# Two graph layers on one core: queries and keys by fifteen block products, and attention under the products around it

## The chip, the core and the metric

The kernel runs on one core of a Trainium2 chip. The core has five engines that run side by side and wait for each other by semaphores: TensorE (PE, matmuls and transposes), VectorE (DVE), ScalarE (ACT), GpSimd (POOL) and SyncE (SP), which issues nearly all the DMA transfers here. Each engine takes its instructions strictly in order, so an instruction that waits holds up all that stand behind it on its engine. The metric is the device time of one execution in microseconds (us); lower is better.

## The reference, cut to what matters

128 graphs have 64 nodes each, with 768 features and an adjacency matrix per graph, all in fp32. Two layers follow each other, each with a residual and a layer norm.

```python
# layer 0: graph attention, 12 heads of 64, and a gate
h    = x @ W                                   # all heads side by side, 768 x 768
th   = tanh(h)
attn = th @ w_src + (th @ w_dst).T             # per head, 64 x 64
attn = softmax(where(adj, leaky_relu(attn, 0.2), -999))
y    = elu(attn @ h + b)
gate = sigmoid(x @ H_w.T + H_b)
x    = layernorm(x + gate * y + (1 - gate) * x)
# layer 1: attention inside a graph, 6 heads of 128
q, k, v = x @ Wq + bq, x @ Wk + bk, x @ Wv + bv
p    = softmax(q @ k.T / sqrt(128) + where(adj, 0, -9e15))
x    = layernorm(x + (p @ v) @ Wf + bf)
```

The 8192 tokens thus pass through six products with a 768 x 768 matrix: h, gate, v, q, k and the output. The change is to q and k, and to the attention of layer 1.

## The kernel before

**Block products.** A product of tokens with a 768 x 768 matrix is cut into blocks of two by two by two. Eight block products would be plain; a Winograd scheme makes do with seven, from sums of blocks of the rows (`block_sums`, L184 to L197) and of the weights (`weight_sums`, L165 to L172). `Job` (L199 to L247) is one such product. `product(i)` issues block product i as three matmuls (its 384 rows of contraction, 128 at a time) into a PSUM bank, some of them onto what is in the bank already; `way_out(i)` reads the bank, by ACT where a result is written first (`first`, `last`) and by DVE where it is added (`add`). `step` (L257) issues a product, then the way out of the product before, so that the reads run one product behind.

**First layer.** Tokens go by pairs of tiles of 128 (32 pairs). The loop at L880 runs one turn per pair, 21 products a turn written out in order (`TURN`, L77): seven for h, seven for the gate, seven for v of the pair before. Everything else of a turn is hung onto positions of that list by `at` and `was` (L891 to L938). The chain through a turn is: h out of PSUM, tanh (L660), its product with the two attention vectors (L661 on DVE, L662 on POOL), a reduction (L669), a round trip through DRAM that turns one of the results into a row (L671, L674), and the logits, mask and exponentials of the 12 heads (L698 to L731), whose transposes stand at the start of the next turn. v waits for row sums of the normed tokens (L192 to L195 on DVE), and the next turn's h and gate for row sums on POOL.

**Passage.** In the last turns (`p == NP - 1`, L940, and `LAST`, L66) the query and key weights are loaded into the places of the first layer's weights as their blocks fall free, and their sums are made on POOL and DVE. `queries_begin` (L870) gives the space of the first layer's rows to the second layer and loads the first group's rows.

**Second layer.** Tokens go by groups of four tiles (512 tokens, 8 graphs; 16 groups). Queries and keys of a group come transposed, features on the partitions. There are three `feature_job`s (L324) per key and group, `fc` = 0 to 2. Each makes 128 features of the lower half and 128 of the upper half, for 512 tokens, in seven products of three matmuls of 256 columns: 63 matmuls per key and group. `attention` (L345) does two heads, those that a feature job has made. It is a generator and goes on one step at each product of the pair of jobs that runs meanwhile (`woven`, L513): load of the values, scores `sp` (16 small matmuls), bias and maximum (L375, L383), exponential, sum and division (L390 to L393), transposes `sT`, context `cp` (32 small matmuls), copy to `ctxT`. A group's loop (L1000 to L1029) has the three pairs of query and key jobs, then the pair of output jobs of the group before. The row sums of a group's tokens are four of 768 columns on POOL (`load_group`, L300). `residuals` (L436) loads the first layer's result, adds the output bias on POOL (L457) and makes the row sums for the output products; `finish` (L497) norms and stores.

There is no scheduler: the order of instructions on each engine is that of the code. A PSUM bank is 128 x 512 fp32; three carry the tag `y`, three `z`, and two `m` (attention and transposes).

Of the kernel before, what the change touches and what calls it, by code (L numbers as in the profile page):

```python
# [9 lines left out]
F32 = mybir.dt.float32  # L10
# [5 lines left out]
P = 128  # L16
# [45 lines left out]
    0: 7, 1: 7, 2: 8, 3: 9, 4: 10, 5: 11, 6: 12, 7: 12, 8: 13, 9: 14, 11: 15, 12: 15, 15: 16, 16: 17, 19: 19,  # L62
# [3 lines left out]
LAST = [  # L66
    "u4", "u3", "q1", "q2", "k1", "k2", "q6", "q5", "q7", "Q1", "q4", "Q2", "q3", "k6", "k5", "k7",
    "Q6", "k4", "k3", "v1", "v2", "v6", "v5", "v7", "K1", "v4", "v3",
]
LAST_REST = [(1, 2), (0, 5), (1, 6), (0, 7), (1, 5), (1, 7), (0, 4), (0, 3), (1, 4), (1, 3)]  # L70
LAST_AT = {3: 3, 4: 4, 5: 6, 6: 8, 7: 9, 8: 11, 9: 12, 11: 15, 12: 16, 15: 20, 16: 20, 19: 22}
# [10 lines left out]
THIRD_AT = {pos: max(pos - 2, 0) for pos in range(len(TURN))}  # L82
# [8 lines left out]
def kernel(  # L91
# [24 lines left out]
    SCALE = 1.0 / math.sqrt(E1)  # L116

# [16 lines left out]
    dst_d = [dram.tile([P, H0], F32, name=f"dstd_{t}") for t in range(2 * NP)]  # L134

# [152 lines left out]
    W2 = PAIR * P  # L288
# [4 lines left out]
    qk, groups = {}, {}  # L293

    def query_tiles(g, fc):
        qk[g, fc] = [
            pools["early"].tile([P, 2, GT * P], F32, tag=f"{k}T", name=f"{k}T_{g}_{fc}") for k in "qk"
        ]

    def load_group(g, eng, between=lambda: None):  # L300

        pool = pools["early"]
        sums = sum_tiles(pool, "sq", W2, f"q{g}")
        between()
        blocks = {}
        for m, kh in ((0, 0), (1, 0), (1, 1), (0, 1)):
            t = pool.tile([P, HK, W2], F32, tag=f"a{m}{kh}", name=f"a{m}{kh}_{g}", bufs=1)
            nc.sync.dma_start(out=t, in_=x1T_d[2 * g + m][:, kh * HK : (kh + 1) * HK, :])
            blocks[m, kh] = t
        groups[g], steps = block_sums(eng, sums, *(blocks[m, kh] for m in range(2) for kh in range(2)))  # L310
        return steps

    def feature_jobs(g, fc):
        return [feature_job(k, groups[g], g, fc, t) for k, t in zip("qk", qk[g, fc])]
# [9 lines left out]
    def feature_job(key, ops, g, fc, dst):  # L324

        w, b = weights[key], bias_c[key]

        def at(m, n):
            return dst[:, n, m * W2 : (m + 1) * W2]

        def bias(n):
            return b[:, n * HK + fc : n * HK + fc + 1]

        return Job(
            f"{key}{g}_{fc}",
            W2,
            lambda i, kc: (w[:, OF_B[i], kc, fc * P : (fc + 1) * P], ops[i][:, kc, :]),
            lambda mn, bk_: S.activation(at(*mn), bk_, AF.Identity, bias=bias(mn[1])),  # L338
            lambda mn, bk_: V.tensor_tensor(at(*mn), bk_, at(*mn), ALU.add),  # L339
            lambda bk_: S.activation(at(1, 0), bk_, AF.Identity, bias=bias(0)),  # L340
        )

    ctxT = {}

    def attention(g, fc, bias):  # L345

        sb = pools["late"]
        qT, kT = qk.pop((g, fc))

        v = sb.tile([P, GT, 2, E1], F32, tag="v1", name=f"v1_{g}_{fc}")  # L350
        for a in range(2):
            c0 = (a * J1 + fc) * E1
            for i in range(GT):
                nc.sync.dma_start(
                    out=v[a * N : (a + 1) * N, i, :, :],
                    in_=v_d[GT * g + i][:, c0 : c0 + E1].rearrange("(g m) e -> m g e", m=N),
                )
        yield
        yield
        yield  # L360
        sp = bank("m", f"sp_{g}_{fc}")
        for i in range(GT):
            for a in range(2):
                for gr in range(2):
                    at = slice(i * P + gr * N, i * P + (gr + 1) * N)
                    T.matmul(
                        sp[gr * N : (gr + 1) * N, (i * 2 + a) * N : (i * 2 + a + 1) * N],
                        qT[:, a, at],
                        kT[:, a, at],
                        start=True,  # L370
                        stop=True,
                    )
        yield
        sc = sb.tile([P, GT, 2, N], F32, tag="sc", name=f"sc_{g}_{fc}")
        V.tensor_tensor(  # L375
            sc,
            sp.rearrange("p (i a m) -> p i a m", i=GT, a=2),
            bias.unsqueeze(2).to_broadcast([P, GT, 2, N]),
            ALU.add,
        )  # L380
        sc3 = sc.rearrange("p i a m -> p (i a) m")
        mx = small.tile([P, 2 * GT], F32, tag="mx1", name=f"mx1_{g}_{fc}")
        V.tensor_reduce(mx, sc3, AX.X, ALU.max)  # L383
        yield
        V.tensor_tensor(sc3, sc3, mx.unsqueeze(2).to_broadcast([P, 2 * GT, N]), ALU.subtract)  # L385
        S.activation(sc, sc, AF.Exp, scale=SCALE)  # L386
        yield
        yield
        den = small.tile([P, 2 * GT], F32, tag="den1", name=f"den1_{g}_{fc}")
# [46 lines left out]
    def residuals(g, last):  # L436
# [14 lines left out]
        if last:  # L451
            sums = sum_tiles(early, "sq", W2, f"o{g}")
# [634 lines left out]
```

## Time and profile before

| | |
|---|---|
| median of 3 runs | 2970.18 us (2967.41 to 2971.54) |
| the profiled execution, its own time | 2970.77 us |
| its span in the profile | 2969.0 us |
| mean granted clock of TensorE | 0.995 |
| PE, DVE, ACT, POOL busy | 2925.2, 1796.9, 1009.0, 811.1 us |
| a turn of the first layer | 45.6 us |
| a group of the second layer | 90.5 us |

The profile is of one execution. Its lines name the source line, the engine, the operation, what is written and what is read (out<-in), how often, and how long. Every fp32 matmul leaves two records, so x576 stands for 288 matmuls. In a group's line the first number after the bar is busy time in us, the second the mean of one in ns, and after the second bar stands the idle time of the engine just before, with what ended it. Line numbers are those of the kernel before.

### The profile page before, as it was taken

To read this page: it belongs to the slowest core of one execution; us is meant where nothing else is said; L and a number is where in the kernel's file an instruction comes from. 1 tells how busy PE (TensorE), PEld (TensorE's weight loads), DVE (VectorE), ACT (ScalarE), POOL (GpSimd) and SP (SyncE) were. 2 spreads that over 40 slices of the span, in tenths; PEclk is the share of its full clock that TensorE was granted. 3 is DMA by queue.
4 is the path that set the end of the run, shared out by engine and by line. 5 is a ranking of instruction groups with operands and counts; after the bars stand their busy time and mean duration, and the time that the engine had idled before them with its cause. 6 is when DMAs were issued, how large, how long until landed. Compare 5 with 4: busy or idle time off the path is not lost.

```text
span 2969.0 us, 45314 instructions
## 1 busy us (share of the span) xinstructions
PE 2925.2 (99%) x18048; PEld 2023.0 (68%) x18048; DVE 1796.9 (61%) x3017; ACT 1009.0 (34%) x1761; POOL 811.1 (27%) x650
## 2 busy tenths in 40 slices
PE   7999999999999999999999999999999999999999
PEld 4566666666666666666578777787777887777875
DVE  6878888788788878887844344333343443443345
ACT  2344344444443444444422222222222222222221
POOL 2434333333343333333422212211111212121121
PEclk9999999999999999999999999999999999999999
DMA  5333333334333333343532211222212222112221
GB/s 171 122 109 114 107 121 115 103 118 128 104 119 104 121 113 106 115 129 103 176 97 77 70 60 55 86 86 76 68 52 64 86 76 73 59 57 82 87 80 48
DMA packets 179681, 284.81 MB, mean 96 GB/s; under 512 B 46736, under 2 KB 113296, under 8 KB 179472
## 3 DMA queue, kind: packets, MB, share of 16 engines
q1 hardware_dynamic: 179472, 281.93, 29.1%
q8 instruction: 143, 2.34, 0.3%
q14 instruction: 66, 0.54, 0.1%
HBM read 167.81 MB, written 101.06 MB: 91 GB/s over the span
## 4 chain that ended last, share of the span: by engine, by line
PE 94%; DVE 3%; DMA 1%; ACT 1%; issue 0%; SPq 0%; POOLq 0%; POOL 0%; DVEq 0%; ACTq 0%
PE y_k L222 8%; PE y_o L222 8%; PE y_q L222 8%; PE y_v L222 8%; PE y_h L222 8%; PE y_g L222 8%; PE z_v L222 4%; PE z_o L222 4%; PE z_k L222 4%; PE z_h L222 4%; PE z_q L222 4%; PE z_g L222 4%; PE x_k L222 2%; PE x_o L222 2%; PE x_q L222 2%; PE x_h L222 2%
## 5 line engine op out<-in xcount | busy, mean ns | idle before, releaser
L789 POOL TENSOR_TENSOR x<-gate,x 128x768 f32<-128x768 f32 x64 | 117.4, 1835 | 323.8 <-ACT gate L840 309.0
L457 POOL TENSOR_TENSOR y<-y,bf_bc 128x768 f32<-128x768 f32 x64 | 115.3, 1832 | 311.4 <-DMA y<-x1d 311.4
L481 DVE TENSOR_TENSOR y<-y_o,y 128x384 f32<-128x384 f32 x128 | 71.4, 557 | 202.1 <-PE y_o L222 198.0
L339 DVE TENSOR_TENSOR kT<-z_k,kT 128x256 f32<-128x256 f32 x96 | 40.8, 425 | 239.3 <-PE z_k L222 136.1
L662 POOL TENSOR_TENSOR th<-th,wsd 128x768 f32<-128x768 f32 x64 | 117.2, 1832 | 182.5 <-DVE th L661 182.5
L274 POOL TENSOR_TENSOR rs_b<-ve_b,minus_half 128x1 f32<-128x1 f32 x64 | 35.1, 548 | 452.5 <-DVE ve_b L272 451.7
L192 POOL TENSOR_TENSOR sq_q<-a,a 128x768 f32<-128x768 f32 x16 | 29.2, 1828 | 432.8 <-PE y_o L222 286.9
L222 PE MATMUL y_h<-w_wq,xT 128*128 128x384 f32 x384 | 136.3, 492 | 8.6 <-DMA w_wq<-in_w_dram 7.9
L222 PE MATMUL y_k<-a,hw_wk 128*128 128x256 f32 x576 | 144.6, 387 | 0.0
L222 PE MATMUL y_q<-a,w_wq 128*128 128x256 f32 x576 | 140.9, 381 | 1.9 <-ACT qT L338 1.9
L222 PE MATMUL z_v<-wv,sv_v 128*128 128x384 f32 x384 | 138.9, 498 | 3.2 <-DVE v L652 3.2
L222 PE MATMUL y_q<-sq_q,w_wq 128*128 128x256 f32 x576 | 140.3, 380 | 0.9 <-ACT qT L338 0.9
L222 PE MATMUL y_h<-w_wq,sx_x 128*128 128x384 f32 x384 | 136.5, 492 | 4.2 <-ACT h L622 4.2
L222 PE MATMUL z_q<-sq_q,w_wq 128*128 128x256 f32 x576 | 140.1, 379 | 0.0
L222 PE MATMUL y_k<-sq_q,hw_wk 128*128 128x256 f32 x576 | 140.1, 379 | 0.0
L222 PE MATMUL z_k<-sq_q,hw_wk 128*128 128x256 f32 x576 | 140.0, 379 | 0.0
L338 ACT ACTIVATE qT<-y_q,bq_c 128x256 f32<-128x256 f32 x144 | 67.4, 469 | 213.2 <-PE y_q L222 213.2
L222 PE MATMUL y_v<-wv,sv_v 128*128 128x384 f32 x384 | 136.6, 492 | 3.0 <-DVE sv_v L193 3.0
L386 ACT ACTIVATE sc<-sc 128x512 f32<-128x512 f32 x48 | 30.2, 630 | 319.3 <-DVE sc L385 319.3
L222 PE MATMUL z_h<-w_wq,sx_x 128*128 128x384 f32 x384 | 137.6, 495 | 0.9 <-DVE w_wq L168 0.9
L222 PE MATMUL y_g<-hw_wk,sx_x 128*128 128x384 f32 x384 | 134.9, 488 | 2.4 <-DVE hw_wk L171 2.2
L222 PE MATMUL y_v<-wv,x1T 128*128 128x384 f32 x384 | 136.1, 491 | 1.2 <-ACT x1T L739 1.0
(171 smaller groups left out, 6678.1 us busy)
## 6 DMA issues: line engine op xcount, KB each, us to landing
x<-in_x_dram SPq DMA_DIRECT2D x64, 384.0 KB, 3.6
dd<-dstd SPq DMA_DIRECT2D x128, 192.0 KB, 3.4
x1d<-x SPq DMA_DIRECT2D x64, 384.0 KB, 2.6
x1Td<-x1T SPq DMA_DIRECT2D x32, 768.0 KB, 4.8
vd<-v SPq DMA_DIRECT2D x64, 384.0 KB, 2.9
a<-x1Td SPq DMA_DIRECT2D x64, 384.0 KB, 3.6
v<-vd SPq DMA_DIRECT2D x384, 64.0 KB, 2.3
y<-x1d SPq DMA_DIRECT2D x64, 384.0 KB, 4.1
```

The costliest lines, as they stand in the source:

```text
L192: lambda: e.tensor_tensor(s1, a21, a22, ALU.add),
L222: T.matmul(to[:, : self.n], lhsT, rhs, start=kc == 0 and not more, stop=kc == HK - 1, skip_group_check=more,)
L274: G.tensor_tensor(rstd, ve, minus_half, ALU.pow)
L338: lambda mn, bk_: S.activation(at(*mn), bk_, AF.Identity, bias=bias(mn[1])),
L339: lambda mn, bk_: V.tensor_tensor(at(*mn), bk_, at(*mn), ALU.add),
L386: S.activation(sc, sc, AF.Exp, scale=SCALE)
L457: G.tensor_tensor(y, y, pools["bf"], ALU.add)
L481: V.tensor_tensor(at(*mn), b, at(*mn), ALU.add)
L662: G.tensor_tensor(th[:, 1, :], th[:, 1, :], wsd[:, 1, :], ALU.mult)
L789: G.tensor_tensor(xp, st[t]["gate"], xp, ALU.mult)
```

## The change

Queries and keys of a group are now made by a scheme for blocks of three by three by two: the weights in 3 x 3 blocks of 256 x 256, the group's tokens in two halves of 256. Eighteen block products would be plain; the table `WIDE` does it in fifteen. A row of it has the path (which PSUM bank the product goes to, onto what is there), the sum of weight blocks, the row operand (a block, or a sum of two, one of which can be an earlier sum), and where the bank is read to. A block product is four matmuls of 256 columns: 60 per key and group. What follows from it:

- The sums of weight blocks are made during the first layer's turns (`sum_weights`): blocks loaded by SP, added on POOL, stored to DRAM. In the last turn they are loaded (`load_wide`) into the places that fall free (`PLACE`).
- The row sums are eleven of 512 columns on POOL, made four products ahead (`Rows.ready`). The next group's row blocks are loaded as they fall free (`NEXT_X`).
- `way_out` writes 256 columns by ACT and adds 512 by DVE.
- Queries and keys of a group are interleaved, and all of a group's three pairs of heads go by a table of ticks (`TICKS`), one tick per product: mostly under the output products of the group before, and on under the next group's query and key products. The query, key and context tiles have one buffer each. In the first group the queries run with the first layer's last v product (`LAST`) and the keys alone after it; the last group has ticks of its own.
- Heads are paired as 2f, 2f+1; `gated` has a position of its own (7.5) in the last turn; the output weights are loaded in steps.

```diff
+WIDE = [
+    (0, [(1, 2, -1)], ((0, 0), ALU.add, (1, 0)), [(2, 0, -1)]),
+    (3, [(2, 0, 1)], ((1, 1), ALU.subtract, (2, 1)), [(0, 1, -1)]),
+    (1, [(1, 1, 1), (0, 0, -1)], ((1, 0), ALU.subtract, (1, 1)), [(1, 0, 1)]),
...
+    (2, [(0, 1, 1), (0, 2, 1), (0, 0, -1), (1, 2, -1)], (0, 0), [(2, 0, 1)]),
+]
+PLACE = [0, 1, 2, 3, 9, 10, 7, 8, 11, 12, 13, 14, 4, 5, 6]
+NEXT_X = {5: [(1, 0)], 6: [(0, 0)], 10: [(1, 1), (0, 1)], 13: [(2, 1), (2, 0)]}
+LAST = (
+    ["u4", "u3"]
+    + [f"q{n}" for n in (0, 1, 2, 3, 4, 5, 6, 8, 7, 9, 10, 11, 12)]
+    + ["v1", "v2", "v6", "q13", "v5", "v7", "q14", "v4", "v3"]
+)
...
+PARTS = ("v", "sp", "sc", "ex", "mult", "sT", "scT", "cp", "ctx")
+TICKS = [
+    (0, 1, 2, 3, 5, 6, 7, 15, 16),
+    (3, 4, 5, 6, 8, 9, 10, 19, 20),
+    (16, 7, 8, 9, 11, 17, 18, 22, 23),
+]
+TICKS_0 = [
+    (0, 0, 0, 1, 2, 3, 4, 6, 7),
+    (0, 0, 0, 2, 4, 5, 6, 10, 11),
+    (8, 0, 0, 3, 6, 8, 9, 14, 15),
+]
+TICKS_N = [
+    (0, 1, 2, 3, 5, 6, 7, 9, 10),
+    (3, 4, 5, 6, 8, 11, 12, 14, 15),
+    (10, 7, 8, 9, 11, 16, 17, 19, 20),
+]
...
+    def sum_weights(pool):
+        for key, src in (("q", wq), ("k", wk)):
+            for n, (_, blocks, *_) in enumerate(WIDE):
+                if blocks[0][2] > 0 and len(blocks) == 1:
+                    continue
+                for kc in range(2):
...
+                    acc = pool.tile([P, W2], F32, tag="wacc", name=f"wacc_{key}{n}_{kc}", bufs=1)
+                    nc.sync.dma_start(out=acc, in_=block(*blocks[0][:2]))
+                    for k, f, sign in blocks[1:]:
+                        t = pool.tile([P, W2], F32, tag="wadd", name=f"wadd_{key}{n}_{kc}_{k}{f}", bufs=1)
+                        nc.sync.dma_start(out=t, in_=block(k, f))
+                        yield
+                        yield
+                        yield
+                        G.tensor_tensor(acc, acc, t, ALU.add if sign > 0 else ALU.subtract)
...
+                    nc.sync.dma_start(out=wide_d[key][n][:, kc, :], in_=acc)
...
+    class Rows:
+        def ready(self, upto):
+            for n in range(self.made, min(upto + 1, NW)):
+                x = WIDE[n][2]
+                if len(x) == 3:
+                    t = pools["early"].tile([P, 2, W2], F32, tag="xs", name=f"xs_{self.g}_{n}", bufs=6)
+                    G.tensor_tensor(t, self.of(x[0]), self.of(x[2]), x[1])
+                    self.sums[n] = t
+                self.made = n + 1
...
+    class Wide:
+        def product(self, n):
+            path = WIDE[n][0]
+            more = path in self.banks
+            if not more:
+                self.banks[path] = bank("z" if path else "y", f"{'z' if path else 'y'}_{self.name}_{n}", 3)
+            w, x, b = wide_place(self.key, n), self.rows.operand(n), self.banks[path]
+            for half in range(2):
+                for kc in range(2):
+                    T.matmul(
+                        b[:, half * W2 : (half + 1) * W2],
+                        w[:, kc, half * P : (half + 1) * P],
+                        x[:, kc, :],
...
+        def way_out(self, n):
+            path, _, _, reads = WIDE[n]
+            b = self.banks[path]
+            for f, t, sign in reads:
+                at = self.dst[:, 2 * f : 2 * f + 2, t * W2 : (t + 1) * W2]
+                if (f, t) in self.written:
+                    V.tensor_tensor(at, at, b.rearrange("p (h t) -> p h t", h=2),
+                        ALU.add if sign > 0 else ALU.subtract)
+                    continue
+                self.written.add((f, t))
+                for half in range(2):
+                    S.activation(at[:, half], b[:, half * W2 : (half + 1) * W2], AF.Identity,
+                        bias=bias_c[self.key][:, 2 * f + half : 2 * f + half + 1], scale=float(sign))
...
+    def attention(g, ticks):
+        heads = [Attention(g, f) for f in range(HK)]
+        for tick in range(max(max(t) for t in ticks) + 1):
+            for part in range(len(PARTS)):
+                for head, t in zip(heads, ticks):
+                    if t[part] == tick:
+                        getattr(head, PARTS[part])()
+            yield
...
             if p == NP - 1:
-                q_sums = weight_sums(G, w0_w)[:2] + weight_sums(V, w0_w)[2:]
-                k_sums = weight_sums(G, hw_w)
-                for pos, block in ((2, B11), (3, B21), (8, T3), (15, B22)):
-                    at(pos, True, do(load_block, wq, w0_w, block))
-                for pos, block in ((6, B11), (9, B21), (19, T3), (19, B22)):
-                    at(pos, True, do(load_block, wk, hw_w, block))
-                at(16, True, q_sums[0])
-                at(18, True, queries_begin, q_sums[1])
-                at(19, True, lambda: all_of(row_sums[:2]))
+                at(2, True, do(load_wide, "q", wq, range(4)))
+                at(8, True, do(load_wide, "q", wq, range(4, 8)))
+                at(12, True, do(load_wide, "q", wq, range(8, NW)))
+                at(9, True, do(load_wide, "k", wk, range(4)))
+                at(15, True, do(load_wide, "k", wk, range(4, 8)))
+                at(18, True, queries_begin)
+                at(20, True, do(load_wide, "k", wk, range(8, NW)), lambda: jobs["rows"].ready(2))
...
+                if 2 <= p < NP - 1:
+                    next(summing, None)
+                if item[0] == "q":
+                    jobs["rows"].ready(int(item[1:]) + 4)
...
+        for n in range(NW):
+            step(keys, n)
+            rows.ready(n + 4)
+            next_rows(0, n)
+            next(masking, None)
+        attend, done = attention(0, TICKS_0), nothing
+        for g in range(1, NG):
...
+            for n in range(NW):
+                for key in "qk":
+                    step(pair[key], n)
+                    for s in sides:
+                        next(s, None)
...
+                rows.ready(n + 4)
+                next_rows(g, n)
+            drain(*sides)
+            attend = attention(g, TICKS_N if last else TICKS)
+            if last:
+                attend = chain(attend, residuals(g, True))
+            p = 2 * g - 2
+            woven((out_job(p), out_job(p + 1)), *[attend] * (1 + last))
```

## The prediction

> **What bounds the kernel now.** I read the busy table first, then the chain that ended last, then busy time by stretch, then that chain in order of time, and last the groups of instructions.
>
> ```profile
> PE 2925.2 (99%) x18048; PEld 2023.0 (68%) x18048; DVE 1796.9 (61%) x3017; ACT 1009.0 (34%) x1761; POOL 811.1 (27%) x650
> ...
> PE 94%; DVE 3%; DMA 1%; ACT 1%; issue 0%; SPq 0%; POOLq 0%; POOL 0%; DVEq 0%; ACTq 0%
> ```
>
> TensorE is 99% busy and 94% of the last chain, so a matmul less is time less wherever nothing else becomes late. Busy time alone does not say that PE runs at its peak; the next view does. It shows stretches: PE busy, weight loads, DVE, ACT, POOL, granted clock, DMA share.
>
> ```profile
> 1414.00:1460.00 46.00, 46.00 (x248) 27.91 (x248) 37.31 (x56) 20.42 (x33) 16.93 (x15) 1.00 0.49 160
> 1460.00:1490.00 30.00, 22.52 (x118) 13.55 (x117) 27.72 (x26) 10.73 (x18) 18.68 (x8) 0.94 0.61 205
> 1490.00:1506.00 16.00, 14.14 (x96) 11.35 (x95) 13.53 (x18) 4.78 (x10) 9.48 (x5) 0.82 0.07 26
> 1547.00:1637.00 90.00, 87.23 (x779) 74.06 (x771) 35.48 (x60) 26.87 (x60) 15.16 (x8) 0.98 0.33 100
> 1818.50:1909.00 90.50, 90.50 (x637) 70.63 (x636) 35.77 (x80) 22.92 (x46) 16.46 (x12) 1.00 0.22 71
> ```
>
> Row 5 is one group of the second layer: 90.50 us without a gap at full clock, with DVE at 40%. Row 1 is one first-layer turn, also without a gap, but there DVE is at 81%. Rows 2 to 4 are the passage between the layers: 7.5 + 1.9 + 2.8 = 12.2 us of PE idle, and a lowered clock. The chain, in order of time, names the passage's culprits and gives the price of a product:
>
> ```profile
> 1482.59 2.19 DVE sq_q L195
> 1484.79 2.88 DVE w_wq L170
> ...
> 1488.98 2.40 DVE w_wq L171
> ...
> 1508.60 1.29 PE y_k L222 x6
> ...
> 2904.61 3.87 PE y_o L222 x12
> ```
>
> Row and weight sums of the query stand in DVE's queue ahead of work PE needs. A query or key product of three matmuls (six records, two to a matmul) takes 1.295 us, 0.432 each; an output product 1.94. A group adds up: 42 x 1.295 + 14 x 1.94 = 81.6, and three attentions (scores 1.08, transposes 0.44, context 1.09, about 0.2 twice for the product after them) make 9.0: 90.6 against 90.50. Rows of the groups that I price from (out<-in, count, busy, mean ns):
>
> ```profile
> L339 DVE TENSOR_TENSOR kT<-z_k,kT 128x256 f32<-128x256 f32 x96 | 40.8, 425 | 239.3 <-PE z_k L222 136.1 <-ACT kT L338 103.2
> L375 DVE TENSOR_TENSOR sc<-sp,bias 128x512 f32<-128x512 f32 x48 | 33.2, 692 | 29.6 <-PE sp L366 29.5
> L192 DVE TENSOR_TENSOR sv_v<-x1T 128x384 f32<-128x384 f32 x32 | 41.0, 1281 | 0.0
> L192 DVE TENSOR_TENSOR so_o<-ctxT 128x384 f32<-128x384 f32 x30 | 17.8, 593 | 0.0
> L192 POOL TENSOR_TENSOR sx_x<-xT 128x384 f32<-128x384 f32 x32 | 41.2, 1289 | 8.0 <-DMA xT<-in_xT_dram 8.0
> L193 POOL TENSOR_TENSOR sq_q<-sq_q,a 128x768 f32<-128x768 f32 x16 | 29.5, 1846 | 1.3
> ```
>
> The two DVE rows of L192 are the same sum, 1281 ns with POOL adding beside it and 593 ns mostly without: POOL work can lengthen DVE work.
>
> **What the Trainium skill says.** "TensorE: Matmul & The Clock Gate", section Back-to-back issue gap, gives N/2.4 + 2.5 ns; with the four passes that "FP8 and Floating Point Precision", TensorE Precision Notes, names for true FP32 (the trace shows two records to a matmul, not the passes) my estimate for 256 columns is 0.43 us. The trace agrees with 0.432, so the time goes by columns and not by how they are grouped. The first page's Part 1, The HAM clock gate, says that about 3.4 us of idleness halves the clock; the trace shows 0.82 from 1490 to 1506 us, after the stalls. "GPSIMD Engine Reference", section 3.1, has a two-input add 1.96 times as long as VectorE's; here 1.83 against 0.96 us for 128x768, which agrees.
>
> **The change, part by part.**
>
> *Matmuls.* Per key and group 3 x 7 x 3 = 63 matmuls of 256 columns become 15 x 4 = 60. Over 16 groups and two keys that is 2016 - 1920 = 96 fewer, x 0.432 = **-41.4 us**. All else on PE keeps count and size.
>
> *Way out and row sums in a group (L338, L339, L192 to L195).* ACT keeps 24 copies of 0.47. DVE has 20 adds of 512 columns in place of 18 of 256: 20 x 0.692 - 18 x 0.425 = +6.2 us, so 42 of 88 us. POOL has 11 sums of 512 columns (estimate 1.24 us, two thirds of 1.846) for four of 1.82: 13.6 for 7.3. I cost these at nothing. A sum is issued four products ahead, 8 x 1.73 = 13.8 us, against at most two bias adds (L457, 3.7 us), a wait for their load (landing median 4.1) and itself: 9 us. A bank is written again at the earliest two products later, three steps of 1.73 = 5.2 us between, for a read of 0.7 to 0.95. Uncovered, a late sum would stop PE for its 1.24 us.
>
> *Attention of a group under the products.* Three heads' scores now follow the output products one tick per product. PE's tightest wait is the first head's transpose (tick 6). Behind the second head's scores (tick 4) DVE does that head's bias and maximum (0.69 + 0.69), then the first head's sum, reciprocal and product (0.68 + 0.20 + 0.74): 3.0 us, while PE does two products, 3.9. Margin 0.9 us, so nothing; 0 to +1.5 a group for the range. The value loads keep their count; the third head's eight wait on SP for the first head's context, at tick 16, and are wanted at tick 22, over 10 us later. Behind them on SP stand output stores and the next rows, wanted later still.
>
> *Weight sums move into the first layer.* 84 adds and 4 negations of 128x256 on POOL (estimate 0.61 to 0.8 us from the rows of 768 and 384 columns), with 132 loads and 48 stores on SP at about 0.45 us of issue. They need 456 steps of 21 a turn, so 22 turns: four POOL operations (2.7 us) and eight transfers a turn. POOL has 29 us free in a turn and SP long gaps. Queued behind an add on POOL are the tanh product (L662), the bias add (L685, before the exchange of heads) and the next turn's row sums; behind SP's store, which waits for POOL, the destination terms (L671, L674). Slack in the turn at 961 us: DVE's L193 ends at 1006.46 and PE's product on it starts at 1006.58, only 0.1 us; the first tile's probabilities are 1.5 us early. Most adds fall outside that chain. I take 0.1 us a turn, **+2 us**; from 0 to 0.5 a turn (11).
>
> *The passage.* The weight sums of query and key (two 1152-column sums on DVE in the chain, six on POOL) and DVE's two row sums leave it. In come two 256 KB row blocks and one POOL sum ahead of the first query product. SP now issues seven query weight loads before the destination terms of the last turn: from 1445 us some 5.1 MB, at the 370 GB/s seen there about 14 us, to 1459; the first destination terms left at 1457.35, so they land about 2 us later. But L193, 2.85 us there because of POOL's weight sum, is short again and gives PE 1.5 back. Following the queues on from there I find PE at the first query product about 2 us earlier than before, and further on stalls of 1 to 2 us in place of the 2 to 3 us ones. Of the 12.2 us and the slow clock I give back 9.5: **-9.5 us**; bounds -14 and +8. The first group's keys run alone, one step of 1.73 between write and read of a bank, read 0.95 at most: nothing.
>
> *The end.* In the last group the three heads run two ticks a product. From the first scores' end to the first transpose PE has three products and one score block, 6.9 us; DVE can start the second head's bias only after 5.0 us and needs 1.4 + 1.6 more: 8.0. About 1.1 us stall, and three residual ticks outside cover: **+1.5 us**, 0 to 5.
>
> Sum: 2969.0 - 41.4 - 9.5 + 2 + 1.5 = 2921.6 us of span. The profiled execution took 2970.77, 1.8 more than its span, and the median of the runs is 2970.18, 0.6 less: **2922.8 us**.
>
> **Rivals.** (1) *The passage gives nothing back*: the new loads and POOL sums cost what the old weight sums did. For it: 5.1 MB ahead of small transfers; against: fewer DVE instructions. Passage +4 in place of -9.5: 2936. (2) *Steady stalls*: attention's transposes or POOL's sums are late by 1.5 us in each of 15 groups. For it: margins of 0.9 us; against: DVE under half busy. +22: 2945. (3) *Slower*: the weight sums break the first layer. Each POOL add stops PE for its own 0.65 us, through L661, L669, L192, L193, where slack is 0.1 us. 88 x 0.65 = 57 in place of 2: 2978. It decides from 49 us, 0.56 us per operation. Against: most adds are issued at other places of the turn. (4) *It doesn't do what it says*, the stream being bound by weight loads or rows rather than columns: loads fall in the same proportion and are 68% busy, so unlikely; 2970.
>
> **How the numbers follow.** Likeliest case 0.70 (its own range 2911 to 2931), rival 1 0.12, rival 2 0.10, rival 3 0.06, rival 4 0.02. The range 2910 to 2944 leaves out part of rival 2, rivals 3 and 4 and the tails. About 0.2% (6 us) is what a measurement of this kernel can tell from no change: faster 0.92, same 0.02, slower 0.06.
>
> **What would show it.** A middle group of 87.9 us with no PE wait; 1920 matmuls of 256 columns at the old mean. First-layer turns of 45.6 to 45.7 us between turns 2 and 23; longer ones, with PE waiting on DVE's L193, are rival 3. PE idle under 6 us from the end of the last turn to the first output product; 15 us would be rival 1. PE waits of the transposes on DVE or of query products on POOL in each group are rival 2. I would be wrong above all if a queue that I followed by hand has a wait that I did not see.

## The result, and the profile after

The changed kernel takes 2927.77 us (median of four runs, 2927.07 to 2928.59) against 2970.51 us of the kernel before beside it (2967.41 to 2971.54): a ratio of 0.9858, with a 95% interval from 0.9841 to 0.9875. The prediction was 2922.8 us, with a range from 2910 to 2944. The profiled execution took 2928.25 us and its span is 2926.4 us, 42.6 us less than the 2969.0 of before; the prediction's sum was 2921.6.

The busy table of the changed kernel, and the first line of its last chain:

```profile
PE 2881.9 (98%) x17856; PEld 1984.6 (68%) x17856; DVE 1927.0 (66%) x3045; ACT 988.4 (34%) x1761; POOL 1020.8 (35%) x857
...
PE 85%; DVE 9%; ACT 2%; DMA 2%; issue 1%; POOL 0%; SPq 0%; POOLq 0%; DVEq 0%; ACTq 0%
```

PE's busy time fell by 43.3 us, about as much as the span. But PE is now 85% of the chain in place of 94%, and DVE 9% in place of 3%: the chain leaves PE more often. Busy time by stretch (PE, weight loads, DVE, ACT, POOL, granted clock, DMA share, GB/s):

```profile
1394.80:1440.40 45.60, 45.60 (x247) 27.69 (x247) 36.91 (x54) 20.01 (x33) 16.54 (x15) 1.00 0.38 120
1465.00:1490.00 25.00, 20.56 (x61) 11.27 (x59) 16.60 (x21) 9.18 (x15) 4.75 (x4) 0.93 0.72 236
1490.00:1506.00 16.00, 15.27 (x159) 12.73 (x160) 10.85 (x18) 7.99 (x16) 15.49 (x12) 1.00 0.49 184
1440.33:1623.76 183.43, 176.17 (x1135) 135.54 (x1129) 103.91 (x157) 57.47 (x115) 77.25 (x55) 0.99 0.43 142
1623.92:1711.84 87.92, 87.92 (x626) 68.36 (x625) 44.75 (x81) 21.64 (x46) 24.82 (x19) 1.00 0.23 73
```

The last row is one group of the second layer: 87.92 us without a gap, 2.58 less than the 90.50 of before; that is six matmuls of 0.43. The first row is a late first-layer turn, again 45.60 us without a gap. The row above the last is the passage, from early in the last full turn to the first output product: PE is idle for 7.3 us of it, all of them after 1476 us. From 1490 to 1506 us the clock was 0.82 before and is 1.00 here; the changed kernel's slow stretch lies in row 2. Four groups of instructions whose durations the prediction had to estimate or carry over (out<-in, count, busy, mean ns):

```profile
L440 PE MATMUL z_q<-xs,w_wq 128*128 128x256 f32 x896 | 213.5, 381 | 0.3 <-POOL xs L404 0.3
L455 DVE TENSOR_TENSOR qT<-qT,z_q 128x512 f32<-128x512 f32 x96 | 65.8, 685 | 235.2 <-PE z_q L440 235.1
L404 POOL TENSOR_TENSOR xs<-r,r 128x512 f32<-128x512 f32 x112 | 155.1, 1402 | 100.0 <-PE z_k L440 64.7 <-DMA r<-x1Td 28.6 <-PE y_k L440 6.6
L362 POOL TENSOR_TENSOR wacc_q<-wacc_q,wadd_q 128x256 f32<-128x256 f32 x42 | 36.5, 870 | 51.6 <-DMA wadd_q<-in_wq_dram 43.9 <-DMA dstd<-sd 4.1 <-DMA wacc_q<-in_wq_dram 2.3
```

A matmul record of 256 columns takes 379 to 382 ns (before 379 to 392), and there are 3840 of them, two to each of 1920 matmuls. POOL's row sum takes 1.40 us (estimate 1.24), its weight add 0.87 (estimate 0.61 to 0.8). PE's waits, first from 90 to 1440 us, then from 1440 to 1640, then from 1640 to the end (engine and line that waited, what it waited for: total, times, longest):

```profile
PE y_v L271 <- DVE sv_v L242: 4.3, 9, 0.8
...
PE pTp L920 <- DVE fo L958: 1.5, 9, 0.2
...
PE pTp L920 <- DVE rden L957: 0.6, 2, 0.4
```

```profile
PE y_v L271 <- ACT v L833: 2.8, 2, 2.0
PE sT L550 <- DVE sc L545: 2.0, 1, 2.0
PE pTp L920 <- ACT prob L909: 1.5, 1, 1.5
PE y_q L440 <- POOL xs L404: 0.6, 1, 0.6
```

```profile
PE sT L550 <- DVE sc L545: 1.0, 1, 1.0
```

In the first layer the value product waits nine times for DVE's second row sum (L242, the kernel before's L193; there twice, 1.6 us in all). The transposes wait for DVE eleven times (L957, L958; 2.1 us), which from 90 to 1440 us they did not do before. After 1640 us one wait is left in 1286 us, at the end.

To compare kernels by stage, four marks are read from PE's timeline: A, the start of the first-layer product y_h that follows a wait of 4.2 us for ACT at the start-up; B, the start of the product z_v that ends a value job near 1440 us, early in the last full turn; C, the first output product; D, the last group's first scores. All times are us, from one profile of each kernel.

| kernel | A | A to B, first layer | B to C, passage | C to D, groups | D to the end |
|---|---|---|---|---|---|
| before | 56.89 | 1375.41 | 204.99 | 1331.71 from C to the end | |
| changed | 58.44 | 1381.89 | 183.43 | 1232.81 | 69.83 |
| e1_no_adds | 58.62 | 1374.99 | 184.43 | 1232.81 | 69.85 |
| e2_double_adds | 57.38 | 1386.68 | 183.10 | 1232.82 | 69.82 |
| e3_away | 57.21 | 1375.94 | 183.98 | 1232.81 | 69.86 |
| e4_small_first | 58.46 | 1381.84 | 181.08 | 1232.80 | 69.92 |
| e5_early_transpose | 58.13 | 1380.04 | 184.89 | 1249.87 | 69.87 |
| e6_short_lead | 56.82 | 1380.27 | 182.74 | 1232.81 | 69.86 |
| e7_rows_first | 58.01 | 1381.00 | 178.03 | 1232.81 | 69.85 |
| e8_all | 58.33 | 1374.19 | 175.22 | 1232.81 | 69.65 |
| e9_three_at_12 | 56.69 | 1412.31 | 183.46 | 1232.81 | 69.73 |
| e10_three_at_9 | 58.85 | 1378.07 | 183.88 | 1232.81 | 69.79 |
| e11_best | 58.58 | 1374.09 | 175.80 | 1232.81 | 68.62 |

The table also shows how far one profile can be trusted. Kernels whose code is the same in a stage differ there by up to 2.2 us in A (56.7 to 58.9), by 1.9 in the first layer (the changed kernel, e4 to e7: 1380.0 to 1381.9) and by 2.2 in the passage (182.7 to 184.9), but by 0.02 in the groups.

### The profile page after: what moved, and what is told of

It is laid out like the page before. It is cut to its first block, busy times and chain, and to the rows that moved or that the text cites. A ratio compares the mean times of both kernels' runs of the same rounds, so it can differ in the third digit from the quotient of the medians.

```text
span 2926.4 us, 45671 instructions
## 1 busy us (share of the span) xinstructions
PE 2881.9 (98%) x17856; PEld 1984.6 (68%) x17856; DVE 1927.0 (66%) x3045; ACT 988.4 (34%) x1761; POOL 1020.8 (35%) x857
## 4 chain that ended last, share of the span: by engine, by line
PE 85%; DVE 9%; ACT 2%; DMA 2%; issue 1%; POOL 0%; SPq 0%; POOLq 0%; DVEq 0%; ACTq 0%
PE z_k L440 9%; PE y_o L271 9%; PE z_q L440 8%; PE y_h L271 8%; PE y_g L271 6%; PE y_v L271 6%; PE y_q L440 6%; PE y_k L440 6%; PE z_o L271 4%; PE z_h L271 4%; PE z_v L271 3%; PE z_g L271 2%; PE x_o L271 2%; PE x_g L271 2%; PE cp L569 2%; PE sp L514 2%
## 5 line engine op out<-in xcount | busy, mean ns | idle before, releaser
L455 DVE TENSOR_TENSOR qT<-qT,z_q 128x512 f32<-128x512 f32 x96 | 65.8, 685 | 235.2 <-PE z_q L440 235.1
L440 PE MATMUL z_q<-xs,w_wq 128*128 128x256 f32 x896 | 213.5, 381 | 0.3 <-POOL xs L404 0.3
L639 POOL TENSOR_TENSOR y<-y,bf_bc 128x768 f32<-128x768 f32 x64 | 123.6, 1952 | 246.4 <-DMA y<-x1d 246.4
L440 PE MATMUL z_k<-xs,hw_wk 128*128 128x256 f32 x840 | 200.0, 381 | 0.0
L404 POOL TENSOR_TENSOR xs<-r,r 128x512 f32<-128x512 f32 x112 | 155.1, 1402 | 100.0 <-PE z_k L440 64.7
L440 PEld LDWEIGHTS z_q<-xs,w_wq 128*128 128x128 f32 x896 | 167.5, 190 | 23.6 <-POOL xs L404 0.7
L440 PEld LDWEIGHTS z_k<-xs,hw_wk 128*128 128x128 f32 x840 | 158.3, 190 | 21.9
L323 POOL TENSOR_TENSOR rs_a<-ve_a,minus_half 128x1 f32<-128x1 f32 x64 | 35.9, 562 | 340.9 <-DVE ve_a L321 340.9
L843 DVE TENSOR_TENSOR th<-th,wsd 128x768 f32<-128x768 f32 x64 | 67.7, 1057 | 103.5 <-ACT th L842 103.5
L271 PE MATMUL z_g<-hw_wk,sx_x 128*128 128x384 f32 x384 | 134.4, 486 | 0.0
```

What stands on the lines that cost most here:

```text
L271: T.matmul(to[:, : self.n], lhsT, rhs, start=kc == 0 and not more, stop=kc == HK - 1, skip_group_check=more,)
L323: G.tensor_tensor(rstd, ve, minus_half, ALU.pow)
L404: G.tensor_tensor(t, self.of(x[0]), self.of(x[2]), x[1])
L440: T.matmul(b[:, half * W2 : (half + 1) * W2], w[:, kc, half * P : (half + 1) * P], x[:, kc, :], start=half == kc == 0 and not more, stop=k ...
L455: V.tensor_tensor(at, at, b.rearrange("p (h t) -> p h t", h=2), ALU.add if sign > 0 else ALU.subtract,)
L639: G.tensor_tensor(y, y, pools["bf"], ALU.add)
```

## The experiments

**The weight sums in the first layer.** Theory: POOL's adds lengthen DVE's row sums of the value product, and PE waits for those. The first kernel leaves out the adds and negations and keeps their transfers, the second has every add twice, the third keeps the adds away from five positions of a turn.

```diff
 # e1_no_adds
-                        G.tensor_tensor(acc, acc, t, ALU.add if sign > 0 else ALU.subtract)
...
-                        G.tensor_scalar(acc, acc, -1.0, None, ALU.mult)
 # e2_double_adds, after the add
+                        G.tensor_tensor(t, acc, t, ALU.add)
 # e3_away
-                if 2 <= p < NP - 1:
+                if 2 <= p < NP - 1 and pos not in (10, 11, 12, 13, 14):
                     next(summing, None)
```

> The changed kernel without the 84 adds and 4 negations of weights on POOL in the first layer; all their loads and stores on SP stay. The weights of the query and key products are then not the sums, so the output is another one. My theory (POOL's adds lengthen DVE's row sums of the value product, PE waits for these): turns between 109 and 1440 us go back from 45.6 to 46.1 to 45.6 us, no wait of PE on DVE's L242 above 0.1 us, the stretch up to the last turn 6 to 7 us shorter, time about 2921. Rival A (the 132 loads and 48 stores on SP delay other transfers): no change, 2928. Rival B (the lateness is a start-up matter): no change between 200 and 1440 us.

> The changed kernel with each of the 84 weight adds on POOL followed by a second one of the same size into the tile that is then free; 73 us more of POOL work in the first layer. My theory with a slope by operation (0.075 us of PE for each add): 6 to 7 us longer, 2934. Rival 3 of the prediction, in its mild form (once an add meets the tight chain it stops PE for its whole 0.86 us): the stalls more than double, 15 to 30 us longer, 2943 to 2958. Rival A (transfers): no change, 2928.

> The changed kernel, in which the weight sums advance at 16 of a turn's 21 positions: not at positions 10 to 14, which put an add between the tanh products and the bias add on POOL, right ahead of DVE's row sums of the value product. 464 steps in 29 turns for the 456 needed. My theory (only adds at those places hurt): the 3 to 4 us of PE waits on DVE's L242 go, 2 to 3 us of waits of the transposes on DVE's L957 and L958 stay; time about 2924. Rival (every add hurts by its share of DVE's time, wherever it stands): the same sum of waits at other places, 2928.

Measured: 2922.51, 2931.65 and 2921.61 us, one run each, as for every kernel here but e8_all and e11_best. By stage, the first layer of e1 is 1374.99 us, 5.0 to 6.9 less than in the five kernels with the same adds, and as long as before (1375.41). So the adds cost 6 us, and their 132 loads and 48 stores, which e1 keeps, cost nothing that can be seen: rival A falls. Rival B falls too: of PE's waits on L242 only those at 98 and 141 us are left, which the changed kernel has as well, and from 200 to 1400 us PE does not wait at all. In e2 the first layer is 1386.68, another 4.8 to 6.6 us for 84 adds: some 0.07 us of PE to an add, as the slope had it, and far from the 15 to 30 us of rival 3's mild form. In e3 all 88 operations are there, and the first layer is 1375.94: the place takes away 4 to 6 of the 6 us. I expected only the waits on L242 to go and 2924; the waits of the transposes fell as well, from 2.1 to 1.6 us.

PE's waits in the first layer of e3_away:

```profile
PE pTp L920 <- DVE fo L958: 0.9, 5, 0.2
PE pTp L920 <- DVE rden L957: 0.7, 2, 0.4
PE y_v L271 <- DVE sv_v L242: 0.6, 1, 0.6
```

**The same number of adds at one place.** Two kernels leave out the weight sums and their transfers altogether (query and key weights are single blocks), and do three adds on a spare tile in each of 29 turns, at one position: 12, between the tanh product and the bias add on POOL, or 9.

```diff
...
-        summing = sum_weights(sb)
+        spare = [sb.tile([P, W2], F32, name=f"spare_{i}", bufs=1) for i in range(2)]
...
-                if 2 <= p < NP - 1:
-                    next(summing, None)
+                if 2 <= p < NP - 1 and pos == 12:      # e10_three_at_9: pos == 9
+                    for _ in range(3):
+                        G.tensor_tensor(spare[0], spare[0], spare[1], ALU.add)
```

> The changed kernel without its weight sums and their transfers (query and key weights are then single blocks, the output another one); in place of them POOL does three adds of 128x256 on a spare tile in each of the turns 2 to 30, all three at position 12, between the tanh product and the bias add: 87 adds for the 88 of the changed kernel. Without any adds and with the transfers kept the time was 2922.5. Theory of the place: from the two runs before, the share of adds at positions 10 to 14 (88 x 5/21 = 21) cost 6 us, 0.28 us each; 87 x 0.28 = 25 us, 2947; in the limit of rival 3 of the prediction (each add stops PE for its 0.86 us), 75 us, 2997. Rival (an add costs 0.075 us wherever it stands): 6.5 us, 2929.

> The kernel of e9_three_at_12 with the three adds at position 9, right after the second tile's small POOL operation of the norm, where DVE and POOL both are idle for 2.5 to 4 us. Theory of the place: 0 to 3 us, 2922 to 2925.5. Rival (an add costs 0.075 us wherever it stands): 2929, the same as e9_three_at_12. If the three adds (2.6 us) run into the tanh product of the same tile, 0.3 us a turn: 2931.

Measured: 2956.80 and 2925.18 us. At position 12 PE waits in every turn, at position 9 once, in the first of these turns (2.7 us), and never after. PE's waits from 90 to 1440 us, of e9_three_at_12 and then of e10_three_at_9:

```profile
PE y_v L271 <- DVE sv_v L242: 33.1, 29, 1.2
```

```profile
PE y_v L271 <- DVE sv_v L242: 2.7, 1, 2.7
```

The first layer is 1412.31 us against 1374.99 of e1: 37.3 us for 87 adds, 0.43 each, above the 0.28 expected and under the 0.78 that such an add takes in the next view. (One of the 29 waits, at 96 us, comes before the first add, and the last turn's, 1.18 us, comes after 1440 us.) DVE's and POOL's timeline in one turn of e9 (start, duration) shows the link:

```profile
508.27 2.35 POOL L1157 TENSOR_TENSOR spare<-spare,spare 128x256 f32<-128x256 f32 x3
510.58 3.64 POOL L867 TENSOR_TENSOR h<-h,b_bc 128x768 f32<-128x768 f32 x2
```

```profile
510.71 1.97 DVE L241 TENSOR_TENSOR sv_v<-x1T 128x384 f32<-128x384 f32 x1
512.72 1.92 DVE L242 TENSOR_TENSOR sv_v<-sv_v,x1T 128x384 f32<-128x384 f32 x1
514.55 0.55 DVE L834 TENSOR_TENSOR v<-x_v,v 128x384 f32<-128x384 f32 x1
```

The adds do not run beside the row sums at all. They end before them, but push back POOL's two bias adds. In e10 the last of these reaches only 0.9 us into the first row sum (in the turn before, POOL's pair runs from 458.78 to 462.11 us and L241 starts at 461.23); here the pair, from 510.58 to 514.22 us, stands beside both sums. Between 155 and 1400 us the mean of the first two row sums is 1.96 and 1.92 us here, and 1.31 and 1.23 in both e1 and e10; a sum of this size that mostly has no POOL work beside it, L244, takes 0.55. PE stands at the product that reads the second sum (514.78 us, after a wait of 1.19). The Trainium skill, "SBUF — State Buffer", Terms, says why the two collide: DVE and GpSimd share one pair of ports, locked by one of them for a whole instruction. The trace agrees: L241 and L242, with both operands in SBUF, are long, and L834, which reads one from PSUM while POOL works beside it, keeps its 0.55 us. The ends fit a lock too: L242 ends 0.42 us after the bias adds (514.64 and 514.22 us), and in e10 each of the two sums ends 0.42 us after the POOL instruction beside it.

**The loads of the passage.** The chain of the changed kernel in its last turn, in order of time:

```profile
1463.68 1.66 DVE sd L851
1465.34 0.19 DVE gate L820
1465.53 4.81 DMA dstd<-sd
...
1470.87 4.87 DMA dd<-dstd
...
1475.83 1.51 DVE att L880
```

The store of 6 KB of destination terms holds its read back by 4.82 us (1465.53 to 1470.35), where it was 1.46 in the kernel before (1457.35 to 1458.81). Ahead of it on SP stand seven query weights and four key weights. The Trainium skill, "DMA: Bandwidth & Descriptors", Queues, rings and completion order, says that descriptors of one ring are taken in order; the trace agrees, with a small store behind 256 KB loads more than three times as late.

```diff
 # e4_small_first
-                at(12, True, do(load_wide, "q", wq, range(8, NW)))
-                at(9, True, do(load_wide, "k", wk, range(4)))
-                at(15, True, do(load_wide, "k", wk, range(4, 8)))
+                at(15, True, do(load_wide, "q", wq, range(8, NW)))
                 at(18, True, queries_begin)
-                at(20, True, do(load_wide, "k", wk, range(8, NW)), lambda: jobs["rows"].ready(2))
+                at(20, True, do(load_wide, "k", wk, range(NW)), lambda: jobs["rows"].ready(2))
 # e7_rows_first: the query weights behind the row blocks instead
-                at(18, True, queries_begin)
+                at(18, True, queries_begin, do(load_wide, "q", wq, range(8, NW)))
```

> The changed kernel, in which the last first-layer turn loads the query weights 8 to 14 after its destination terms (position 15 in place of 12) and all key weights after the row blocks (position 20 in place of 9, 15 and 20). My theory (the two transfers of the destination terms, 4.8 and 4.9 us, stand behind 3 MB of weights): each takes 1.5 to 2.5 us, the attention terms of the last tile begin about 5 us earlier, the three PE stalls of 2.0, 1.5 and 0.9 us between 1476 and 1488 us go, in part to later waits on POOL's row sums; 2 to 4 us gained, 2924 to 2926. Rival (DVE's and ACT's chain sets these stalls): no change, 2928. Second rival (key weights come too late for the first group's keys): PE waits for a key weight, slower, 2930 to 2935.

> The kernel of e4_small_first with the last turn's query weights 8 to 14 loaded after the row blocks (position 18 in place of 15). In e4 the row blocks landed at 1485.4 us behind those weights, and PE waited 2.5 us for the first row sum. My theory: the row blocks land 2 to 3 us earlier, that wait goes, the passage is 2 to 2.5 us shorter than in e4, 4 to 5 shorter than in the changed kernel, time about 2923.5. Rival (the row blocks wait for the store of the last transposed tile, not for weights): the same wait, 2926. Second rival (the weights are now late for product 8): PE waits on a weight load, 2926 to 2930.

Measured: 2925.87 and 2921.48 us. In e4 the store is 1.41 us ahead of its read (1465.34 to 1466.75), the last tile's attention term starts at 1476.16 in place of 1481.22, and the stalls on ACT's L833 and L909 are gone. The passage is 181.08 us, 2.4 less than in the changed kernel, which is about the spread of this stage; in their place stand new ones, above all that of the first query product for a row sum, whose rows came behind the weights:

```profile
PE y_q L440 <- POOL xs L404: 2.5, 1, 2.5
PE sT L550 <- DVE sc L545: 2.0, 1, 2.0
PE z_v L271 <- DVE v L834: 0.8, 1, 0.8
```

In e7 the wait of 2.5 us is gone too, and the passage is 178.03 us, 5.4 less than in the changed kernel, outside the spread. So the theory of e7 holds, and its two rivals fall: PE waits neither for a row sum nor for a weight there. The order of the loads alone, with no byte less, is worth 4.7 to 6.9 us. Not all of it is idle time of PE. From B to C, of the kernel before and then of e7:

```profile
1432.30:1637.29 204.99, 192.88 (x1359) 147.84 (x1354) 112.17 (x170) 65.28 (x127) 54.77 (x29) 0.97 0.34 112
1439.01:1617.04 178.03, 173.98 (x1136) 134.97 (x1129) 104.27 (x157) 57.36 (x115) 76.14 (x55) 1.00 0.44 146
```

PE is idle for 4.1 us in e7, 7.3 in the changed kernel and 12.1 in the kernel before. The rest is the clock. Read in windows of 1 us, it falls to 0.50 from 1484 to 1488 us in the changed kernel, behind the stalls of 2.0, 1.5 and 0.9 us, and not at all in e7; in the kernel before it does so four times. Summed over its windows, each of these spells falls 1.7 us short of full clock, and that is my estimate of its cost. So of e7's 5.4 us some 3.2 are idle time and 1.7 the clock.

**The covers in the groups.** The prediction costed the attention under the products and POOL's row sums at nothing, with margins. One kernel takes one product of 1.94 us out of the first head's margin (a head stands here for one of a group's three pairs of heads), the other halves POOL's lead.

```diff
 # e5_early_transpose, first row of TICKS
-    (0, 1, 2, 3, 5, 6, 7, 15, 16),
+    (0, 1, 2, 3, 5, 5, 7, 15, 16),
 # e6_short_lead, in the loop over groups
-                rows.ready(n + 4)
+                rows.ready(n + 2)
```

> The changed kernel with the first head's transpose one output product earlier (tick 5 in place of 6) in the 14 groups that use TICKS. The prediction's margin was 0.9 us between DVE's product and PE's transpose. If that is right, PE comes 1.94 us earlier and waits 1.0 us on DVE's L545 once a group: 14 us longer, 2942, each group 88.9 to 89.0 in place of 87.92. Rival (DVE has more room than I worked out, or other work moves up): no wait, 2928. Second rival (the wait also delays what DVE does next, and other waits follow): over 1.5 us a group, over 2949.

> The changed kernel with POOL's row sums in the groups issued two products ahead in place of four: 6.9 us of lead in place of 13.8. The prediction worked out 9 us at worst (two bias adds of 3.7, a wait for their load of 4.1, the sum itself 1.24). If that cover is needed, PE waits on POOL's L404 for up to 2.2 us where a bias add of L639 stands in front, twice or four times in a group: 0.5 to 4 us a group, 2935 to 2990. Rival (the bias adds' loads have landed by the time POOL reaches them, the worst case is 3.7 to 5.2 us): no wait, 2928.

Measured: 2944.57 and 2924.31 us. PE's waits of e5 in the groups (1625 to 2870 us):

```profile
PE sT L550 <- DVE sc L545: 14.4, 14, 1.0
```

Fourteen waits of 1.03 us: 1.94 less 1.03 is a margin of 0.91, where the prediction had 0.9. The groups became 17.1 us longer (1249.87 against 1232.81), 1.22 each, 0.19 more than the wait. In e9 too a turn grows by 0.14 us more than its wait (37.3 us for 33.2 us of added waits in 29 turns); why, no run shows. For e6 the rival is right: the groups take 1232.81 us to the hundredth, with no wait. The cover of 9 us at worst was not needed, and at a lead of 6.9 there is still enough. That e6 came out 3.5 us faster than the changed kernel is no gain of its edit: all of it lies ahead of C, where its code is the same.

**All of it together.** e8_all joins e3_away and e7_rows_first, with the first group's transposes two to three ticks later and the last group's first transpose one tick later; e11_best keeps the last group's transpose, and moves the second head's bias and maximum one tick down instead.

```diff
 TICKS_0 = [
-    (0, 0, 0, 1, 2, 3, 4, 6, 7),
-    (0, 0, 0, 2, 4, 5, 6, 10, 11),
-    (8, 0, 0, 3, 6, 8, 9, 14, 15),
+    (0, 0, 0, 1, 2, 5, 6, 8, 9),
+    (0, 0, 0, 2, 4, 7, 8, 11, 12),
+    (9, 0, 0, 3, 6, 9, 10, 15, 16),
 # TICKS_N in e8_all
-    (0, 1, 2, 3, 5, 6, 7, 9, 10),
+    (0, 1, 2, 3, 5, 7, 8, 10, 11),
-    (10, 7, 8, 9, 11, 16, 17, 19, 20),
+    (11, 7, 8, 9, 11, 16, 17, 19, 20),
 # TICKS_N in e11_best, instead
-    (3, 4, 5, 6, 8, 11, 12, 14, 15),
+    (3, 4, 6, 7, 8, 11, 12, 14, 15),
```

> A version meant to be faster than both: the changed kernel with the weight sums kept away from positions 10 to 14 (as in e3_away), the order of loads in the last turn of e7_rows_first, the first group's transposes two to three ticks later and the last group's first transpose one tick later. By stages: first layer -6, passage -4.5, the first group's wait of 2.0 us and the last group's of 1.0 us gone: 2928 - 13.5 = about 2914.5. If the gains of the passage are not additive with an earlier end of the first layer, 2917; if later transposes push the context products past their cover, 2918.

> The kernel of e8_all with the last group's ticks as in the changed kernel, except that the second head's bias and maximum come one tick later (6 in place of 5), behind the first head's product on DVE. In e8 the first transpose one tick later only exchanged the wait on DVE for one of 1.0 us on ACT's L595. Theory: DVE ends the first head's product 1.4 us earlier, the wait of 1.0 us of that transpose goes, no other comes; 1 us less than e8_all, 2911.8. Rival: the bank is not free before ACT's copy of the context of the group before, whatever DVE does: 2912.8.

Measured: e8_all 2912.78 us (2911.93 to 2914.35, four runs), 0.9814 of the kernel before, from 0.9798 to 0.9831. e11_best 2911.71 us (2909.64 to 2913.44, five runs), 0.9807, from 0.9793 to 0.9820. The parts add up: in e11 against the changed kernel 7.8 us from the first layer, 7.6 from the passage, 1.2 from the end, 16.5 of span in all. In e8 the later transpose only took a new wait for the old one:

```profile
PE sT L550 <- ACT ctxT L595: 1.0, 1, 1.0
```

In e11 no wait of the transpose is left and the end is 1.2 us shorter than in the changed kernel (68.62 against 69.83); by the medians the two versions cannot be told apart.

## Why the prediction was right, and where it was off

The kernel became faster, for the reason named, and the time lies 5.0 us over the forecast and inside the range. Step by step, with the sum's terms in the order of the span:

- *Matmuls, -41.4.* Right. A group is 87.92 us, the 87.9 predicted, with no PE wait in 14 groups. Rival 4 falls. That the time goes by columns, as the prediction took from the skill's price, is what a product of 1.73 us for four matmuls of 256 columns, in place of 1.295 for three, shows. (Small slips in the working: 96 x 0.432 is 41.5, the estimate for a matmul of 256 columns comes by its own terms to 0.44 us and not 0.43, and the slack read as 0.12 us in the turn at 961 us is 0.14, as PE starts at 1006.60. Together they move the sum by 0.1 us.)
- *DVE, ACT and POOL in a group at nothing.* Right: e5 finds the margin of 0.91 us, and e6 more cover for POOL than was worked out. DVE is busy for 44.75 of a group's 87.92 us rather than 42. Its row sums of the output operands take 1.06 us, the last of four 0.81, where they took 0.55 to 0.60, and POOL has more to do in these groups. The timelines of two groups (1624 to 1800 us) show that the one comes with the other: of sixteen such sums the thirteen with POOL at work beside them take 0.82 to 1.77 us, the three without it 0.55. Rival 2 falls.
- *Weight sums in the first layer, +2.* This is the term that was mis-sized. It measures 5.0 to 6.9 us (the five kernels with these adds, against e1), inside the 0 to 11 given. The failing step is "Most adds fall outside that chain. I take 0.1 us a turn": an add need not fall into the chain. Of the nine waits on L242, the two at 98 and 141 us stand in e1 too. The other seven, of 0.25 to 0.54 us and 3.0 in all, each have an add ahead of POOL's bias adds or between them, which moves these onto DVE's row sums: the first sum takes 1.77 to 1.99 us there, where a turn without an add at this place has 1.30. In four further turns the first sum takes 1.99 us and PE does not wait: POOL is idle next, and the second sum takes 0.56 us in place of 0.96 to 1.24. The transposes' waits of 2.1 us on DVE, of which e1 has none from 90 us on, come with the adds as well; which adds open them, no run separates. The add also measures 0.87 us instead of 0.61 to 0.8. The prediction looked at the right wait, with the wrong rule for when it opens.
- *Rival 3* named the right mechanism and the right place and was wrong on the size for this order of the work: 88 operations cost 6 us and not 57. e9 shows that it was no idle threat. At the one bad position an add costs 0.43 us, not far under the 0.56 from which it decides; at position 9, beside one wait in the first turn, nothing.
- *The passage, -9.5.* Right in the sum, within the spread, and wrong in a part. From B to C the kernel is 21.6 us shorter. Of that 5.2 are twelve fewer matmuls of two groups, and 6.0 the attention of two pairs of heads, which now comes after C. That leaves -10.4, with one profile of before to compare and a spread of 2.2 us. PE's idle time gives 4.8 of it (12.1 to 7.3), and three half-clock spells fewer, 1.7 us each, about 5.1: the lowered clock, to which the prediction gave no size of its own, is half of the gain. For a halved clock the prediction quotes about 3.4 us of idleness from the Trainium skill ("TensorE: Matmul & The Clock Gate", Part 1, The HAM clock gate); here shorter stalls did it. The longest ahead of a spell is 2.0 us in the changed kernel and 3.2 before, and two spells of before follow a single stall of 1.9. Yet a stall of 2.0 us in e7 has none behind it, so what length decides, these runs do not show. The step "they land about 2 us later" fails: the store's read is held back by 4.82 us in place of 1.46 and the attention terms follow it. It cost about what e7 gets back, some 5 us (up to 0.9 of them waits for row sums, which e7 ends as well), and the rest of the passage gave more than I had worked out. PE is idle for 7.3 us there, where I had put the bound at 6. Two of them are a wait that I had not seen: the first group's transpose on DVE, behind the bias and maximum of all three heads; in e8 and e11, with later transposes, it is gone. Rival 1 falls.
- *The end, +1.5.* Right: one wait of 1.03 us, with the cause named (the second head's bias in front of the first head's sum); e11, which moves that bias, is rid of it. From C to the end, 1331.71 becomes 1302.64; with 84 fewer matmuls (36.3 us) and the 6.0 us of attention, 1.2 are left for the end.
- *Start-up.* Not in the sum. A came 1.55 us later in the changed kernel's profile, but it lies anywhere from 56.7 to 58.9 in kernels that begin with the same code, so it is not laid to the change.

Together 1.55 + 6.5 - 10.4 - 41.5 + 1.2 is -42.6 up to rounding, the measured difference of the spans. The 4.8 us by which the predicted sum is short are 4.5 of the weight sums and 1.55 of the start, less 0.9 of the passage and 0.3 of the end.

## What to carry to other kernels

Work that is put into the gaps of an engine off the critical path is priced by what it pushes, not by what it meets: look at what stands behind it in that engine's queue, and whom that will then collide with, and choose the place by it (the same 87 adds cost 37 us at position 12 of the turns, and 3 at position 9). A small transfer that something waits for goes ahead of the bulk loads of the next stage; here the order alone was worth about 5 us. A stall of PE can cost more than its length, where the clock falls behind it: look at the granted clock beside the idle time. Compare single profiles by stage, and first find out how far stages with the same code differ.

## What the runs showed of the hardware that I had not expected

A DVE sum of 128x384 with both operands in SBUF takes 0.55 us alone and up to 1.97 with POOL working beside it, while DVE's adds with one operand in PSUM keep their time (0.55 for 128x384 beside POOL, 0.69 for 128x512). POOL pays as well: its add of 128x256 takes 0.73 us on a spare tile (mean of e9 and e10). In the changed kernel 63 of 84 take 0.72 to 0.75, and 21 take 0.85 to 2.03, each of these with a DVE instruction of two SBUF operands beside it. A store of 6 KB behind bulk loads on the same queue was waited for during 4.82 us, and 1.41 without them. The granted clock halved for some 3.4 us behind stalls of 1.9 to 3.2 us (1.7 us lacking at half clock), four times from B to C in the kernel before and once in the changed kernel.
